# Gated attention: when the second half of a batch's softmax results is asked for

## The chip, the cores and the metric

One core of a Trainium2 chip. The metric is the time of one execution on the device in microseconds; lower is better. Five engines work side by side, each through its own instructions in order: PE (TensorE, matrix products), DVE (VectorE), ACT (ScalarE), POOL (GpSimd) and SP (SyncE), which computes nothing here and only issues transfers (DMAs). They wait for one another through semaphores.

## The reference

Two layers on 16 batches of 128 tokens with 512 features. The first is a decoder layer (self-attention, cross-attention, an MLP). The second, in whose part of the kernel the change lies, is a gated cross-attention:

```python
a = _layer_norm(audio_kv, ln_gamma, ln_beta)
Q = (hidden_states @ Wq.T) ...   # 16 heads of 32
K, V = (a @ Wk.T) ..., (a @ Wv.T) ...
scores = jnp.einsum('bhtd,bhsd->bhts', Q, K) * scale
scores = jnp.where(mask, scores, -inf)
attn = jax.nn.softmax(scores, axis=-1)
out = jnp.einsum('bhts,bhsd->bhtd', attn, V) @ Wo.T
return hidden_states + jnp.tanh(gate) * out
```

All of it is in float32.

## The kernel before, in words

The work goes in groups of four batches. Self-attention and cross-attention of all groups run first (one call of `attend`), then the MLP, then the gated attention of the four groups D0 to D3 (a second call of `attend`, with `ready=True`). The change is in `attend`; it acts in the second call only.

**Units and steps.** A batch has 16 heads and is cut into four *units* of four heads: unit `4b + j` is `j` of batch `b`, 64 units in the gated run. `attend` writes the instructions step by step, one unit a step, as a pipeline by hand. At step `k`:

- if `k` is a multiple of 4, PE computes the scores of a whole batch (`scores`, into four PSUM banks `sc`);
- DVE masks the scores into SBUF tiles `s` (`scale_unit`, tag `s`, seven buffers), one or two units a step, and finds each row's least value;
- ACT takes the exponentials of unit `k-1` (`exp_unit`), POOL divides unit `k-2` by its sums (`norm_unit`);
- DVE transposes unit `k-3` in squares of 32 and SP sends it to DRAM, 256 KB (`turn_unit`, tile `away_D<-s_D` in the trace);
- SP fetches a pair of units back in four pieces of 128 KB (`receive_pair`, tile `pT_D<-away_D`, tag `pT`, three buffers), which finishes the transposition: the squares land where they belong;
- PE mixes the values of a batch with its four units (`mix`, `av_D` in the trace), one of the two pairs being units `4b`, `4b+1`, the other `4b+2`, `4b+3`.

Each unit is thus sent at step `u + 3`. The dictionaries `mixed_at` and `received_at` say at which step a batch is mixed and a pair received. In the gated run a batch `b` is mixed at step `4b + 10`; its first pair is received at step `4b + 6` (the later unit of it was sent at `4b + 4`), and its second at `4b + 8` (later unit sent at `4b + 6`). The last batch (15) doesn't travel: its units are transposed by PE.

**Order inside a step.** What sets the order on SP is the order in which `step` calls things:

```python
if m == 0 and bt is not None:
    scores(bt)
for pair in pairs:
    receive_pair(*units[pair])
due()
...
for job in jobs:
    job()
...
    ahead.prepare(k % NS)
if 0 <= k - 3 < len(units) and not first_turned:
    (turn_unit if k - 3 < by_transfer(k) else turn_by_array)(*units[k - 3])
```

So a step's receive stands on SP ahead of that step's other transfers, and its send stands last. A receive waits until both sends of its pair have landed in DRAM. SP issues in order: whatever stands behind a waiting receive waits with it. The trace also shows that a DMA is issued only after the one eight places before it has landed (the back_x piece at 999.78 us is issued when the one of 995.10 has landed at 999.76, that of 1000.48 when that of 995.74 has).

**What else travels in the gated run.** While group `g` runs its attention, `jobs` projects Q, K and V of the next group on PE, and `prepare` (class `GatedAttention`) fetches the tokens of the group after that: `hidden_states` sends x turned (`turned_x`, steps 6, 8, 10, 12), and pieces of 256 KB come back at positions 1, 3 (`back_x`) and 7, 9 (`back_a`) of a group's 16 steps, two each time. ACT needs them at positions 5, 6 and 12 to 15. In the third group `deferred_start` fetches earlier groups' mixed results (`mixed`, positions 7, 9, 11, 13) and x (position 15); in the fourth the output is stored. `put_away` stores a mixed result (`kept_mT`), and each group loads a mask (`m`) before its first step.

Of the kernel before, what the change touches and what calls it, by code (L numbers as in the profile page):

```python
# [26 lines left out]
GB = 4  # L27
# [27 lines left out]
def decoder_then_gated_cross_attention(ctx: ExitStack, tc: tile.TileContext, a: dict, out: bass.AP):  # L55
# [24 lines left out]
    def afterwards(engine, do):  # L80
        late[engine].append(do)

    def due():

        left = [do for queue in (late["dve"], late["act"]) for do in queue]
        for queue in late.values():
            queue.clear()
        for do in left:
            do()
# [456 lines left out]
    def scores(bt):  # L546
        sec, t = bt.sec, slice(bt.b * S, (bt.b + 1) * S)
        for j in range(GB):
            bt.sc[j] = ps("sc", f"sc_{bt.name}_{j}")
        for c in range(KC):  # L550
            for j in range(GB):
                r = slice(j * HD, (j + 1) * HD)
                nc.tensor.matmul(
                    bt.sc[j][:, c * S : (c + 1) * S], sec.q[r, c, t], sec.k[r, c, t], start=True, stop=True
                )
# [4 lines left out]
    def by_head(t):  # L560
        return t.rearrange("p n c j -> p c n j")
# [30 lines left out]
    def norm_unit(bt, j):  # L592
        s, sm = bt.s[j], bt.sum.pop(j)
        nc.vector.reciprocal(sm, sm)
        scale = sm.unsqueeze(1).unsqueeze(3).to_broadcast([P, NQ, KC, Q])
        nc.gpsimd.tensor_tensor(s, s, scale, ALU.mult)
# [24 lines left out]
    def receive_pair(bt, j):  # L621

        pT = work.tile([P, NQ, 2, KC, Q], F32, tag="pT", name=f"pT_{bt.name}_{j}", bufs=3)
        for m in range(NQ):
            nc.sync.dma_start(
                out=pT[m * Q : (m + 1) * Q].rearrange("k n u c q -> k n (u c q)"),
                in_=bt.away[j // 2][m].rearrange("(n k) u x -> k n (u x)", k=Q),
            )
        for u in range(2):
            bt.pT[j - 1 + u] = pT[:, :, u]  # L630

    def mix(bt):
        sec, b = bt.sec, bt.b
        av = ps(mixed_in[0], f"av_{bt.name}")
        for c in range(KC):
            for j in range(GB):
                h = c * GB + j
                nc.tensor.matmul(
                    av[j * HD : (j + 1) * HD, c * S : (c + 1) * S], sec.v[:, b, h * HD : (h + 1) * HD],
                    bt.pT[j][:, :, c, :], start=True, stop=True,  # L640
                )
        at_end = work.tile([P, KC, S], F32, tag="s", name=f"mT_{bt.name}", bufs=7) if bt.by_array else None
        mT = bt.mT = sec.mixed_tile(b) if at_end is None else at_end

        def mixed_out():
            if sec.v_bias is None:
                nc.scalar.copy(mT, av.rearrange("p (c q) -> p c q", q=S))
            else:
                for c in range(KC):
                    nc.scalar.activation(  # L650
                        mT[:, c], av[:, c * S : (c + 1) * S], AF.Identity, bias=col(sec.v_bias[0], sec.v_bias[1] + c)
                    )

        return mixed_out

    def out_project_last(bt):

        for n in range(2):
            at_ = slice(n * HF, (n + 1) * HF)
            mm = ps("mm", f"mo_{bt.name}_{n}")  # L660
            for c in range(KC):
                nc.tensor.matmul(
                    mm[:, 0:HF], bt.mT[:, c, :], bt.sec.w_o[:, c, at_], start=(c == 0), stop=(c == KC - 1)
                )
            bt.sec.finish(mm[:, 0:HF], bt.b, at_)

    def out_project(bt):
        mm = ps(mixed_in[0], f"mo_{bt.name}")
        for c in range(KC):
            nc.tensor.matmul(mm, bt.mT[:, c, :], bt.sec.w_o[:, c, :], start=(c == 0), stop=(c == KC - 1))  # L670
        afterwards("dve", lambda: bt.sec.finish(mm, bt.b))
# [13 lines left out]
    def attend(sections, ready, others, after=None):  # L685

        if not ready:
            sections[0].start(sections[1])
        units, batches = [], []
        projected = deque()

        last = (len(sections) * GB - 1) * GB

        def by_transfer(n):

            return min(n, last) if ready else n  # L700

        mixed_at, received_at = {}, {}
        for b in range(len(sections) * GB):
            sooner = 2 if ready else min(2, max(0, b + 4 - len(sections) * GB))
            k, at = (b + 3) * GB - sooner, (b + 2) * GB - max(1, sooner)
            if ready and b * GB == last:
                k = last + 7
            else:
                for half in range(2):
                    received_at.setdefault(at + 2 * half, []).append(b * GB + 2 * half + 1)  # L710
            mixed_at[k] = b

        def step(k, bt=None, jobs=(), ahead=None):

            m = k % GB
            mixed_in[0] = "sc" if not ready and k > last + 2 else "mm"
            pairs, done = received_at.get(k, []), mixed_at.get(k)
            beside_scores = done is not None and m == 0
            if beside_scores:
                mixed_out = mix(batches[done])  # L720
# [5 lines that stand above are left out]
            if beside_scores:  # L726
                mixed_out()
                projected.append((k, batches[done]))
            for job in jobs:
                job()  # L730
            last_mix = ready and k == last + 7
            if last_mix:
                afterwards("act", mix(batches[-1]))
                projected.append((k, batches[-1]))
            if projected and k - projected[0][0] >= (1 if ready and bt is None else 2):
                before = projected.popleft()[1]
                if before.by_array:
                    out_project_last(before)
                elif before.sec.deferred:
                    afterwards("act", lambda: before.sec.put_away(before))  # L740
                else:
                    out_project(before)
            first_turned = ready and k == last + 6
            if first_turned:
                turn_by_array(*units[k - 3])
            if done is not None and not (beside_scores or last_mix):
                mixed_out = mix(batches[done])
                if ready:
                    afterwards("act", mixed_out)
                else:  # L750
                    mixed_out()
                projected.append((k, batches[done]))
            if ahead is not None:
# [3 lines that stand above are left out]
            def norm():  # L757
                if 0 <= k - 2 < len(units):
                    norm_unit(*units[k - 2])

            def exp():
                if 0 <= k - 1 < len(units):
                    least_unit(*units[k - 1])
                    exp_unit(*units[k - 1])


            for do in (exp, norm) if ready else (norm, exp):
                do()
            if bt is not None:
                for j in SCALED[m]:  # L770
                    scale_unit(bt, j)
                if bt.b < sec.by_head_from:
                    bt.sec.add_mask(by_head(bt.s[m]), bt.b)

        k = 0
        for i, sec in enumerate(sections):
            jobs = others() if i + 1 == len(sections) else sections[i + 1].jobs()
            ahead = sections[i + 2] if i + 2 < len(sections) else after if i + 2 == len(sections) else None
            for b in range(GB):
                bt = Batch(sec, b)  # L780
                batches.append(bt)
                for m in range(GB):
                    units.append((bt, m))
                    step(k, bt, jobs.get(k % NS, ()), ahead)
                    k += 1
        while projected or k < len(units) + 2 * GB:
            step(k, jobs=jobs.get(k - len(units) + NS, ()))
            k += 1
# [1038 lines left out]
```

## Time and profile before

| what | value |
|---|---|
| median of 3 runs | 1155.73 us (1155.29 to 1156.04) |
| the profiled execution | 1154.62 us |
| its span, first to last instruction | 1152.8 us |
| its granted TensorE clock | 0.997 |
| busy on PE, DVE, POOL, ACT | 98%, 64%, 60%, 53% of the span |
| queue 1 (all of SP's DMAs) | 258.38 MB, 78.8% of 16 engines' span |
| gated run, first scores to end of the span | 940.7 to 1152.8 us |

The profile is of one execution. Its busy shares say how long each engine worked; the lists of waits say what ended each engine's idle time; the timeline gives instructions in order with their start and length, runs of like ones merged ("x4"), and in brackets the idle time before and what ended it. A DMA's row on SP is the time its issue took; the transfer itself goes on, and the trace has the moment at which each landed.

Where a step of the gated run stands in time: the scores of batches 0 to 15 (steps 0, 4, 8 ...) start at 940.7, 952.4, 963.3, 976.5, 987.7, 1000.6, 1012.4, 1025.7, 1036.8, 1049.7, 1060.8, 1072.0, 1083.1, 1096.0, 1108.9 and 1120.0 us, so a step takes some 2.9 to 3.0 us.

### The profile page before, as it was taken

To read this page: it belongs to the slowest core of one execution; us is meant where nothing else is said; L and a number is where in the kernel's file an instruction comes from. 1 tells how busy PE (TensorE), PEld (TensorE's weight loads), DVE (VectorE), ACT (ScalarE), POOL (GpSimd) and SP (SyncE) were. 2 spreads that over 40 slices of the span, in tenths; PEclk is the share of its full clock that TensorE was granted. 3 is DMA by queue.
4 is the path that set the end of the run, shared out by engine and by line. 5 is a ranking of instruction groups with operands and counts; after the bars stand their busy time and mean duration, and the time that the engine had idled before them with its cause. 6 is when DMAs were issued, how large, how long until landed. Compare 5 with 4: busy or idle time off the path is not lost.

```text
span 1152.8 us, 22191 instructions
## 1 busy us (share of the span) xinstructions
PE 1129.9 (98%) x7246; PEld 873.1 (76%) x7246; DVE 743.4 (64%) x1919; ACT 611.1 (53%) x2142; POOL 694.6 (60%) x633
## 2 busy tenths in 40 slices
PE   9999999999999999999999999999999999999998
PEld 8877777666675757546788888888888877878875
DVE  6678978798787776987564634443342237767754
ACT  3567676767667666774231333233222337877663
POOL 6798888788868685773333414443342168545873
PEclk9999999999999999999999999999999999999999
DMA  6588889999888879999696696697447827888975
GB/s 222 159 211 233 217 221 224 256 240 260 210 225 217 233 217 250 289 285 294 226 258 234 183 283 191 201 274 261 155 154 228 261 59 201 236 253 230 267 220 175
DMA packets 325284, 259.81 MB, mean 225 GB/s; under 512 B 83560, under 2 KB 280624, under 8 KB 320304
## 3 DMA queue, kind: packets, MB, share of 16 engines
q1 hardware_dynamic: 325128, 258.38, 78.8%
q8 instruction: 58, 0.95, 0.4%
q14 instruction: 58, 0.48, 0.1%
q10 hardware_dynamic: 40, 0.01, 0.0%
HBM read 163.94 MB, written 94.37 MB: 224 GB/s over the span
## 4 chain that ended last, share of the span: by engine, by line
PE 71%; DMA 10%; POOL 6%; DVE 5%; ACT 3%; issue 3%; SPq 2%; POOLq 0%; DVEq 0%; ACTq 0%
PE h L51 17%; PE o L51 16%; PE mo_A L51 4%; PE mm_q_B L51 3%; PE mm_v_B L51 3%; PE mo_B L51 3%; PE mm_v_A L51 3%; PE mm_q_A L51 3%; PE mm_v_D L51 3%; PE mm_k_A L51 3%; PE mm_k_B L51 3%; PE mm_q_D L51 2%; DMA away_D<-s_D 2%; POOL x L51 2%; SPq L51 2%
## 5 line engine op out<-in xcount | busy, mean ns | idle before, releaser
L51 DVE TENSOR_TENSOR h<-h,h 128x512 f32<-128x512 f32 x80 | 54.9, 686 | 114.5 <-PE h L51 114.5
L51 ACT ACTIVATE h<-h 128x512 f32<-128x512 f32 x64 | 40.3, 630 | 161.5 <-DVE h L51 161.5
L51 ACT ACTIVATE s_A<-s_A,mn_A 128x128 f32<-128x128 f32 x256 | 99.4, 391 | 46.7 <-issue 24.1
L51 ACT ACTIVATE s_B<-s_B,mn_B 128x128 f32<-128x128 f32 x256 | 99.4, 392 | 31.1 <-issue 18.2
L51 POOL TENSOR_TENSOR s_D<-s_D,sum_D 128x512 f32<-128x512 f32 x64 | 66.5, 1040 | 57.7 <-DVE sum_D L51 52.2
L51 ACT ACTIVATE s_D<-s_D,mn_D 128x128 f32<-128x128 f32 x256 | 99.1, 392 | 0.4 <-issue 0.4
L51 POOL TENSOR_TENSOR s_B<-s_B,sum_B 128x512 f32<-128x512 f32 x64 | 67.1, 1048 | 52.2 <-DVE sum_B L51 38.1
L51 POOL TENSOR_TENSOR s_A<-s_A,sum_A 128x512 f32<-128x512 f32 x64 | 66.7, 1042 | 30.5 <-DVE sum_A L51 23.9
L51 POOL TENSOR_TENSOR s_A<-s_A,ma 128x512 f32<-128x512 f32 x64 | 81.9, 1280 | 5.1 <-DVE s_A L51 4.1
L51 POOL TENSOR_TENSOR s_B<-s_B,mask 128x512 f32<-128x512 f32 x60 | 76.6, 1277 | 2.2 <-DVE s_B L51 1.3
L51 POOL TENSOR_TENSOR rstd_aD<-rstd_aD,mhalf 128x1 f32<-128x1 f32 x12 | 6.6, 550 | 115.1 <-DVE rstd_aD L51 101.6
L51 POOL TENSOR_TENSOR sh<-h 128x512 f32<-128x512 f32 x32 | 40.6, 1270 | 50.6 <-ACT h L51 49.6
L51 PE MATMUL h<-sx,t 128*128 128x256 f32 x256 | 61.9, 386 | 2.0 <-ACT h L51 2.0
L51 PE MATMUL h<-T_C,w 128*128 128x256 f32 x256 | 61.1, 381 | 0.8 <-DVE h L51 0.8
L51 PE MATMUL h<-T_C,t 128*128 128x256 f32 x256 | 60.6, 379 | 1.0 <-DVE h L51 1.0
L51 PE MATMUL o<-w,h 128*128 128x256 f32 x256 | 60.9, 381 | 0.0
L51 PE MATMUL o<-t,h 128*128 128x256 f32 x256 | 60.5, 379 | 0.0
L51 PE MATMUL o<-t,sh 128*128 128x256 f32 x256 | 60.5, 379 | 0.0
L51 DVE CUSTOM_DVE_ANT_0 s_D<-sc_D,gmask 128x128 f32<-128x128 f32 x256 | 57.2, 283 | 2.1 <-DMA turned_x<-x_D 1.2
L51 PE MATMUL mo_B<-w_co,mT_B 128*128 128x512 f32 x128 | 57.6, 593 | 0.0
L51 PE MATMUL mo_A<-w_ao,mT_A 128*128 128x512 f32 x128 | 57.5, 592 | 0.0
L51 PE MATMUL mm_q_B<-T_B,w_cq 128*128 128x512 f32 x128 | 57.4, 596 | 0.0
(335 smaller groups left out, 3002.0 us busy)
## 6 DMA issues: line engine op xcount, KB each, us to landing
t<-kept SPq DMA_DIRECT2D x24, 1024.0 KB, 8.0
away_A<-s_A SPq DMA_DIRECT2D x64, 256.0 KB, 3.1
pT_A<-away_A SPq DMA_DIRECT2D x128, 128.0 KB, 3.5
away_B<-s_B SPq DMA_DIRECT2D x64, 256.0 KB, 4.5
pT_B<-away_B SPq DMA_DIRECT2D x128, 128.0 KB, 3.7
away_D<-s_D SPq DMA_DIRECT2D x60, 256.0 KB, 3.5
pT_D<-away_D SPq DMA_DIRECT2D x120, 128.0 KB, 2.7
w<-in_L_xattn_w_dram SPq DMA_DIRECT2D x24, 512.0 KB, 6.1
```

Of the source, the lines that this page charges most:

```text
L51: return lambda *args, **kw: self.tc.keep_in_program_order(call(*args, **kw))
```

## The change

One line in `attend`. In the gated run (`ready`), the second pair of a batch is received one step after the first instead of two: at step `4b + 7`, not `4b + 8`. That is seven units behind the scores of the batch and one step behind the send of the pair's later unit. The first pair, the mixing and everything else stay where they are; the first call of `attend` is unchanged.

```diff
             else:
                 for half in range(2):
-                    received_at.setdefault(at + 2 * half, []).append(b * GB + 2 * half + 1)
+                    received_at.setdefault(at + (1 if ready else 2) * half, []).append(b * GB + 2 * half + 1)
             mixed_at[k] = b
```

On SP the order between a batch's two receives changes from "first receive, send 4b+3, step 4b+7's transfers, send 4b+4, second receive, send 4b+5, send 4b+6" to "first receive, send 4b+3, second receive, step 4b+7's transfers, send 4b+4, send 4b+5, send 4b+6".

## The prediction

> **What bounds the kernel now.** I read the page's first part, then busy time by stage for the gated run (start 940.7 us, where the first of its scores run), then who waited for whom there on PE and on SP.
>
> ```profile
> PE 1129.9 (98%) x7246; PEld 873.1 (76%) x7246; DVE 743.4 (64%) x1919; ACT 611.1 (53%) x2142; POOL 694.6 (60%) x633
> ```
> ```profile
> 940.00:988.00 48.00, 46.27 (x373) 37.96 (x375) 33.97 (x172) 34.01 (x131) 39.61 (x34) 1.00 0.71 189
> 988.00:1037.00 49.00, 47.02 (x428) 38.69 (x425) 34.07 (x174) 37.12 (x153) 26.40 (x24) 1.00 0.92 249
> 1037.00:1083.00 46.00, 46.00 (x424) 38.26 (x423) 34.62 (x175) 33.67 (x148) 30.54 (x28) 1.00 0.88 244
> ```
> ```profile
> PE av_D L51 <- DMA pT_D<-away_D: 2.5, 4, 1.7
> PE tp_D L51 <- POOL s_D L51: 1.7, 1, 1.7
> ```
> ```profile
> SPq L51 <- DMA away_D<-s_D: 40.5, 28, 3.5
> SPq L51 <- DVE s_D L51: 31.0, 16, 9.8
> ```
>
> PE is the bound: in the gated run it idles about 6 us before its last matmul, and only 2.5 us of that is waiting for softmax results (av is the mix of batch b, at step 4b+10). The last two figures of a stage row are the share of the DMA engines and GB/s: 0.92 and 0.88 in the middle. The second bound is close behind: SP, which issues every DMA in order. Its receives waited 40.5 us, in 28 of 30 cases, for a send to land. It was on time (waiting for DVE to finish a unit) for 16 sends of 60.
>
> The four waits of PE, from its timeline, and SP's queue at the longest:
>
> ```profile
> 971.88 1.07 PE L51 MATMUL av_D<-pT_D,v_D__7856 128*32 128x128 f32 x28 [0.15 <-DMA pT_D<-away_D]
> 1009.49 1.07 PE L51 MATMUL av_D<-pT_D,v_D__7856 128*32 128x128 f32 x28 [0.26 <-DMA pT_D<-away_D]
> 1021.02 1.07 PE L51 MATMUL av_D<-pT_D,v_D 128*32 128x128 f32 x28 [1.72 <-DMA pT_D<-away_D]
> 1140.72 1.94 PE L51 MATMUL av_D<-pT_D,v_D 128*32 128x128 f32 x60 [0.33 <-DMA pT_D<-away_D]
> ```
> ```profile
> 1010.11 1.78 SPq L51 DMA_DIRECT2D pT_D<-away_D  x4
> 1011.99 0.38 SPq L51 DMA_DIRECT2D away_D<-s_D  x1
> 1012.41 1.01 SPq L51 DMA_DIRECT2D back_a<-turned_a  x2
> 1013.52 0.38 SPq L51 DMA_DIRECT2D away_D<-s_D  x1
> 1014.86 2.31 SPq L51 DMA_DIRECT2D pT_D<-away_D  x4
> 1017.28 0.38 SPq L51 DMA_DIRECT2D away_D<-s_D  x1
> ...
> 1021.54 1.73 SPq L51 DMA_DIRECT2D pT_D<-away_D  x4
> ```
> ```profile
> 1011.99 2.81 DMA away_D<-s_D
> ...
> 1016.74 4.04 DMA pT_D<-away_D
> 1021.02 1.07 PE av_D L51 x28
> ```
>
> Units are counted from 0; send n is that of unit n. The rows are batch 4: first receive, send 19, two pieces of the next group, send 20, second receive. The chain of waits (last fence) shows that send 19 landed at 1014.80 and that the second receive was issued at 1014.86, that is on landing. It could not have gone earlier.
>
> **The change, part by part.** No instruction is added, removed or resized on any engine. On SP alone, the four DMAs of each batch's second receive (15 times) move from the head of step 4b+8 to the head of step 4b+7: ahead of send 4b+4 and of whatever else step 4b+7 issues. That is two pieces of back_a or back_x in batches 0, 3 and 4; two of mixed or x in 8, 9 and 10; an output store in 13 and 14; the next mask in 2 and 6; nothing else in 1, 5, 7, 11 and 12. No other queue is passed.
>
> *What goes.* A second receive still waits for send 4b+3 to land, one step behind it now. Sends take 2.2/3.5/5.9 us to land (least, median, most, the tile view of s_D); a step is some 2.9 us. So it goes out hardly earlier; but its transfers overtake those it passed. In batch 4 these are three transfers of 256 KB, each seen to take about 0.7 us of a busy queue (landings 0.64 to 0.81 us apart where it was backed up): about 2 us sooner, which would end the 1.72 us wait. The 0.15 and 0.26 us would go likewise. The 0.33 us at the end would not: its receive (issued 1136.63) waited for send 59, landed 1136.58, and only a store was passed. The most that can be won is 2.1 us.
>
> *What comes.* Everything passed is now queued on SP behind the wait for a landing, plus the four issues (1.75 to 1.9 us). Before, that work filled the wait. Worked out on batch 0: send 3 went at 963.71 and landed at 966.36; two back_a pieces and send 4 (965.77) filled the gap; the receive went at 966.42, an x send at 968.29, send 5 at 968.83. After: the receive again at 966.42 to 968.24, then two pieces (1.1), send 4 at 969.4 (3.6 late), x send, send 5 at 970.3 (1.5 late). The DMA queue has nothing from 966.36 until the receive's first piece; send 5 lands about 974.8 instead of 973.04. The next receive waits for it: 1.8 late; sends 6 and 7 follow it; send 7's landing moves from 980.36 to 982.1, so batch 1's second receive lands at 986.3 instead of 984.50, where mix 1 started at 984.74. That is about 1.5 us on PE, which had none.
>
> Batch 4 the same way: receive at 1014.86, two pieces to 1017.8, send 20 some 4.3 late, send 21 about 1.1 late, the next receive at 1021.65 if the 2.4 us hold-up that the first back_a piece met (5.49 us to land) falls into the empty queue, at about 24.0 if not: 0.1 to 2.5 late. So a laden batch pushes SP back by 0.1 to 2.5 us; I take 1.5, near batch 0's 1.8. An unladen batch leaves the queue idle for about one transfer, 0.7 us.
>
> *The reserve.* From the landings of the second receives and the starts of the mixes, the margin was 0.2 us in batch 1, 1.3 in 2, none in 3 and 4 (they waited), 2.6 in 5, 1.8 to 2.7 in 6 and 7, 0.8, 1.4 and 1.5 in 8 to 10, 2.5 in 11, 3.2 or more in 12 and 13.
>
> *The sum.* Batches 0 to 3 push 1.8+0.7+1.5+1.8 = 5.8 us by mix 4; its own overtaking gives about 2 back, so some 3.8 us more waiting than before by then. Batch 4 pushes another 1.5: SP is 7.3 late at mix 5 against a margin of 2.6, so 4.7 in all; I take 4.5. Batches 5 to 7 recover. Batches 8 to 10 push 4.5, 11 another 0.7, against margins of 1.5 to 2.5: 3 us by mix 11. I add 1.5 for hold-ups that the reserve used to absorb, in the tail too. Together +9. The profiled execution took 1154.62 us (span 1152.8 and 1.8 around it), 1.1 below the median of 1155.73: 1163.6, so I say 1164. With 0.1 a laden batch nearly all fits the margins (within 2 us of before); with 2.5 the eight laden batches up to 10 push 1.0 more each, less some margin: +15.
>
> *A rule against the row.* The row: these sends, 256 KB, landed after 3.5 us in the median and 2.2 at least. The Trainium skill, DMA: Bandwidth & Descriptors, section "Anatomy of one DMA", has a fixed 2.0 us plus bytes over 436 GB/s (fitted on the GpSimd path): an estimate of 2.6 us. By it each wait would be 0.9 shorter, and a sum over these eight batches would lose some 7 of the 9 us. The same section calls the fixed part completion latency: a queue that is emptied before each receive pays it anew, which speaks against the change. The row is measured in this queue, so it decides.
>
> **The rivals.**
> - *SP becomes the bound in the laden stretches (forecast)*: +4 to +14 us. For it: late sends already (send 17 was turned at 1002.03 and issued at 1006.95). Against it: DVE's 31.0 us of SP waits show reserve in the last section. Chance 0.60.
> - *The late sends also block DVE (+14 to +22, 1172)*: a late send keeps its s buffer, one of seven, so the scaling seven units later waits on DVE, and scores, turns and sends with it. For it: DVE waited 1.2 us for an x send and 0.3 us for a send before such scalings (about 980 and 1005), and send 20 had 1.0 us to spare. Against it: margins of 2.5 us and more from batch 7 on. Eight batches at 1 us more: 1172. Chance 0.14.
> - *The passed work has time (not slower)*: send 4b+4 is first needed three steps later. It decides if the push of a laden batch stays under about 0.5 us, so that margins of 0.8 to 2.6 us take it: 1154 to 1157.5. For it: empty queues let transfers land in 2.2 us, and the hold-ups may fall into them. Chance 0.18, within 0.2% nearly all.
> - *All three avoidable waits go and nothing else comes*: 1155.73-2.1 = 1153.6, just within 0.2%; faster than that only if the 0.9 us PE waited for mn_D goes too. Chance 0.08, half of it faster.
>
> **How the numbers follow.** 0.2% (2.3 us) is about what a measurement of this kernel can tell from no change. Slower: 0.60+0.14+0.04 of the third = 0.78; within: 0.18; faster: 0.04. The range, 1154 to 1174, reaches from the third rival's low end to the second's price and leaves out 2 in 10 at most.
>
> **What the profile after would show.** Right: SP's wait for away_D over 50 us; each send 4b+4 two to eight us after its turn; PE waiting for pT_D about 10 us, at mixes 1, 3, 4 and 8 to 11; the gaps of the first mix gone. Wrong: PE's wait for pT_D below 3 us. If instead PE waits for mn_D before scores, and DVE for away_D, the second rival is at work. The stages before 940 us should not change.

## The result and the profile after

The changed kernel took 1167.72 us (median; 1166.72 to 1169.62 in 4 runs) beside 1155.88 us of the kernel before on the same chips: a ratio of 1.0111, 95% interval 1.0091 to 1.0132, slower by 11.8 us in the medians, 12.8 by the ratio. The profiled execution spans 1164.9 us where before's spanned 1152.8. PE's busy time is the same, its share one point lower:

```profile
PE 1130.7 (97%) x7246; PEld 872.2 (75%) x7246; DVE 743.1 (64%) x1919; ACT 611.8 (53%) x2142; POOL 695.3 (60%) x633
```

All of the loss is in the gated run: from its first scores to the end of the span it takes 225.0 us, 12.9 more than before's 212.1. Who waited there, on SP, PE, DVE and ACT (total us, times, longest):

```profile
SPq L51 <- DMA away_D<-s_D: 69.0, 33, 4.3
...
SPq L51 <- DVE s_D L51: 16.2, 6, 9.8
```
```profile
PE mm_k_D L51 <- ACT k_D L51: 5.3, 2, 4.6
PE sc_D L51 <- DVE mn_D L51: 2.0, 3, 0.9
PE mm_o_D L51 <- ACT mT_D L51: 1.8, 1, 1.8
PE av_D L51 <- DMA pT_D<-away_D: 1.4, 2, 0.8
PE tp_D L51 <- POOL s_D L51: 1.3, 1, 1.3
PE mm_v_D L51 <- DVE v_D L51: 1.2, 1, 1.2
PE mm_o_D L51 <- DVE x L51: 0.7, 1, 0.7
```
```profile
DVE s_D L51 <- DMA away_D<-s_D: 9.2, 6, 2.6
DVE x L51 <- DMA x<-kept_x: 6.4, 2, 4.9
```
```profile
ACT T_D L51 <- DMA back_x<-turned_x: 6.3, 1, 6.3
```

SP waits 69.0 us for sends to land (40.5 before) and waits for DVE, that is, is ahead of it, 6 times, not 16. (The counts are of single DMAs: two of before's 28 were not receives but transfers that waited for the DMA eight places before, so 26 belong to receives, not the 28 that the prediction read.) PE waits 13.9 us instead of 5.8, and hardly for pT_D: the 2.5 us of before became 1.4. It waits for ACT and for DVE, and these wait for transfers that SP issued late: DVE 9.2 us for sends that still hold an s buffer (0.3 before), ACT 6.3 us for a back_x piece (0.5 before, at the same place).

Against before's schedule (set equal at the first scores), the scores of batch 4 come 2.6 us late, of batch 6 9.5, of batch 13 11.0, of batch 15 12.6. The largest step, 7.0 us, lies between the scores of batches 5 and 6 (about 1002 to 1021 us), in which batch 4's results are received; it is called the block below. SP's timeline ahead of it, then the chain of work that leads to PE's longest wait, and that wait:

```profile
1000.91 1.73 SPq L51 DMA_DIRECT2D pT_D<-away_D  x4
1002.75 0.38 SPq L51 DMA_DIRECT2D away_D<-s_D  x1
1007.50 1.73 SPq L51 DMA_DIRECT2D pT_D<-away_D  x4
1009.28 0.90 SPq L51 DMA_DIRECT2D back_x<-turned_x  x2
1010.29 0.93 SPq L51 DMA_DIRECT2D away_D<-s_D  x2
```
```profile
1002.75 4.70 DMA away_D<-s_D
...
1009.75 4.29 DMA back_x<-turned_x
...
1015.17 1.63 ACT s_D L51 x8
1016.80 0.48 ACT k_D L51
...
1017.42 3.75 PE mm_k_D L51 x8
```
```profile
1017.42 3.75 PE L51 MATMUL mm_k_D<-T_a,gsums 128*128 128x256 f32 x8 [4.62 <-ACT k_D L51]
```

Send 15 goes at 1002.75. Batch 3's second receive stands behind it now, and SP does nothing for 4.4 us until it has landed. Two back_x pieces, sends 16 and 17 follow at 1009.28 to 1011.2; send 16 had been turned at 1001.42. ACT, in order, stands before the back_x piece from 1007.8 to 1014.1, its exponentials and the copy of k_D behind it; PE wants the bank that this copy frees and idles 4.62 us. Then PE's clock is halved; busy time by stretch (the figure ahead of the last two is the granted clock):

```profile
1016.00:1018.00 2.00, 0.58 (x2) 0.52 (x3) 1.16 (x10) 2.00 (x8) 0.91 (x1) 0.50 0.80 239
1018.00:1022.00 4.00, 4.00 (x24) 2.90 (x26) 2.00 (x4) 3.13 (x13) 1.17 (x2) 0.50 0.55 150
```

The halved stretch lasts 6.83 us (1015.4 to 1022.2); eight matmuls took 3.75 us, not 1.99. Had PE worked all through it, that would be 3.4 us of work lost; PE was idle until 1017.4, so some 2.4 us are. Waits (+8.1) and clock (+2.4) make 10.5 of the 12.9; the rest was not followed.

### The profile page after: what moved, and what is told of

The parts are those of the page before. It is cut to its first block, busy times and chain, and to the rows that moved or that the text cites. A ratio compares the mean times of both kernels' runs of the same rounds, so it can differ in the third digit from the quotient of the medians.

```text
span 1164.9 us, 22210 instructions
## 1 busy us (share of the span) xinstructions
PE 1130.7 (97%) x7246; PEld 872.2 (75%) x7246; DVE 743.1 (64%) x1919; ACT 611.8 (53%) x2142; POOL 695.3 (60%) x633
```

## The experiments

Each edit is against the kernel after, in the line of the diff or near it; times stand beside the kernel before on the same chip, and a loss in us is worked out from the ratio (on about 1156 us). Two theories stood first: A and B both made the block the heart of the loss, the rival C a general lateness that shows where it happens to.

**Only batch 3 moved.**
```diff
-received_at.setdefault(at + (1 if ready else 2) * half, [])...
+received_at.setdefault(at + (1 if ready and b == 3 else 2) * half, [])...
```


> Only batch 3's second receive moves to step 4b+7; the other 14 stay at 4b+8. In the changed kernel ACT waited 6.3 us for the back_x pieces that this receive passes, and PE idled 4.6 us behind it at half clock afterwards. Theory A (the wait is made by lateness that SP gathers over batches 0 to 3, and the passed pieces only hand it to ACT): SP is on its old schedule here, send 15 lands near 1005 as before, the pieces go out about 1007 and land about 1010.3 where ACT wanted them at 1009.7: 0 to +2 us, about 1157. Theory B (the passed pieces alone are the cause): the whole block at 1011 to 1022 returns, +6 to +9 us, about 1163.

1160.29 us beside 1156.19, ratio 1.0046 (1.0028 to 1.0064): about 5 us, between A and B. In its profile ACT waits 3.4 us for back_x, PE 2.83 us behind it, and the clock is halved for 3.41 us:

```profile
ACT T_D L51 <- DMA back_x<-turned_x: 3.4, 1, 3.4
```

The passed pieces hurt even with SP on its old schedule up to there, so the block is real. By the time between the scores of batches 5 and 6 it is 3.3 us in this profile, less than half of the changed kernel's 7.0; the profiled execution was the fastest of six, 1157.25 us. The expectation under A reckoned from a wrong moment. ACT needs all of back_x at position 5, and before the change it already stood waiting for the last piece there:

```profile
1006.60 1.15 ACT L51 ACTIVATE T_D<-back_x 128x512 f32<-128x512 f32 x2 [0.55 <-DMA back_x<-turned_x]
```

So ACT wanted the pieces by 1006.6 at the latest, not at 1009.7 as the expectation had it, and a landing at 1010.3 is some 3.7 us late, about what ACT waits here.

**All but batch 3 moved.**
```diff
+received_at.setdefault(at + (1 if ready and b != 3 else 2) * half, [])...
```


> The change in every batch but 3, whose second receive stays at step 4b+8, behind the back_x pieces. Theory A: SP is still 2 to 4 us late by batch 3, but ACT gets its pieces before the late receive, so the 4.6 us idle of PE and the halved clock go, and some waiting for pT_D comes at mixes 3 and 4 in their place: +4 to +7 us, about 1161. Theory B: only what lies outside the block is left, +3 to +5 us, about 1160. Rival C (every late send costs DVE and PE about the same in each batch, the block is no more than where it shows): nearly nothing is won, +10 to +12 us.

1166.10 us, ratio 1.0101 (1.0079 to 1.0124): 11.7 of the 12.8 us stay, and the difference is within the noise. The 4.6 us wait for k_D is gone (0.7 us is left, as before the change), and others have its place:

```profile
PE av_D L51 <- DMA pT_D<-away_D: 6.4, 5, 1.7
PE sc_D L51 <- DVE mn_D L51: 2.4, 3, 1.1
```

A and B, which made the block the heart of the loss, fall; C's range holds the result. The block takes up lateness that costs about the same elsewhere when it cannot come out there.

**Pieces asked for earlier.**
```diff
-            if p in (1, 3, 7, 9):
+            third = 2 if g == 3 else 3
+            if p in (1, third, 7, 9):
                 for m in range(2):
-                    self.part(m + 2 * (p in (3, 9)))
+                    self.part(m + 2 * (p in (third, 9)))
```


> The changed kernel, with the second two back_x pieces of group 3 asked for one step earlier (position 2 of 16 instead of 3), so that batch 3's receive no longer passes them; they stand ahead of send 15 instead. All 15 receives stay at 4b+7. Theories A and B: ACT's wait of 6.3 us for back_x goes, PE's 4.6 us behind it too, and the halved clock: about +5 us left of the 12, 1160 to 1162. Rival C: 1166 to 1168, since SP has the same work in a slightly other order.

1170.89 us, ratio 1.0139 (1.0116 to 1.0162), if anything worse than the change itself. ACT no longer waits for back_x, but send 15 now follows two more pieces, and PE waits 3.4 us for pT_D at mix 3, with 6.83 us at half clock behind it. A and B fall again; C comes nearest, but the time lies above its range too, and where the excess comes from was not followed.

**The step's other transfers first.**
```diff
-            for pair in pairs:
-                receive_pair(*units[pair])
+            behind = ready and m == GB - 1
+            if not behind:
+                for pair in pairs:
+                    receive_pair(*units[pair])
             due()
...
                 ahead.prepare(k % NS)
+            if behind:
+                for pair in pairs:
+                    receive_pair(*units[pair])
```


> All second receives stand in step 4b+7, but behind the other transfers of that step and ahead of send 4b+4 alone. So the pieces of back_a, back_x, mixed and x fill SP's wait for the landing again; only send 4b+4 is late. Theory A: an unladen batch's push (0.7 us) is left in every batch, less than the margins of the second receives: +0 to +4 us, about 1158. Rival C, in the form that the late sends hold the s buffers and so DVE: send 4b+4 is as late as in the changed kernel, +8 to +12 us.

1160.74 us, ratio 1.0047 (1.0028 to 1.0067): 5.4 of the 12.8 us are left, between the two expectations. More than half of the loss goes when the pieces, masks and stores are no longer passed; what is left comes with sends 4b+4 alone. C in its DVE form is not borne out here: DVE waits 8.1 us for sends, nearly the 9.2 of the changed kernel, but PE's wait for DVE's mn_D is the 0.9 us of before, and PE waits for pT_D instead, 5.2 us at seven mixes.

Theory D came out of these: what costs is SP standing before a landing with nothing left to issue, 15 times, each time about a send's whole landing.

**First receive later, second as before the change.**
```diff
+received_at.setdefault(at + (1 + half if ready else 2 * half), [])...
```


> The second receive back at step 4b+8 as before the change; instead the first receive moves one step later, from 4b+6 to 4b+7. Both its sends have landed by then, so it waits for nothing, and its four issues (1.8 us) and send 4b+4 fill the time in which send 4b+3 lands, for which the second receive waits. Theory D (what costs is SP standing empty-handed in front of a landing, so that sends and pieces behind it run late): SP's wait for sends falls from 40.5 to under 20 us, the 2.5 us that PE waited for pT_D shrink to under 1, nothing else on PE changes: 0.1 to 0.2% faster than before, about 1154.5. Rival E (each receive has a margin of its own, and the first pair's was needed): PE waits more for pT_D, 0 to +4 us.

1156.83 us beside 1155.22, ratio 1.0017 (1.0004 to 1.0029). Slightly slower, where theory D expected slightly faster. SP's wait fell much further than expected, yet the time did not:

```profile
SPq L51 <- DVE s_D L51: 59.2, 32, 9.8
SPq L51 <- DMA away_D<-s_D: 4.9, 9, 1.7
```
```profile
PE av_D L51 <- DMA pT_D<-away_D: 3.4, 2, 2.7
```

At mix 0 PE waits 2.7 us: batch 0's second receive now has the first one and two back_a pieces ahead of it, and its margin was none. E was right at this one place, and SP's wait is not the only thing that counts.

**Both receives at step 4b+7.**
```diff
+received_at.setdefault(at + (1 if ready else 2 * half), [])...
```


> The second receive at step 4b+7 as in the changed kernel, and the first receive at the same step, just ahead of it. The second receive passes just what it passes in the change, but the first one's 1.8 us of issues now fill most of its wait, and sends 4b+3 go out without a receive ahead of them. Theory D: SP's wait for sends is 20 to 35 us, below the 40.5 of before, and the time is that of before within 3 us (1154 to 1159). Rival F (what costs is that the pieces and send 4b+4 stand behind the second receive, whatever SP does meanwhile): they are as late as in the change or later, +8 to +14 us.

1156.01 us, ratio 1.0002 (0.9987 to 1.0017): no loss, with every second receive where the change put it. This decides against F, which expected +8 to +14 us. D's time holds; its figure for SP's wait, 20 to 35 us, was too high. SP's timeline around batch 0, and its waits:

```profile
963.19 0.36 SPq L51 DMA_DIRECT2D away_D<-s_D  x1
963.65 3.87 SPq L51 DMA_DIRECT2D pT_D<-away_D  x8
967.62 0.85 SPq L51 DMA_DIRECT2D back_a<-turned_a  x2
968.57 0.38 SPq L51 DMA_DIRECT2D away_D<-s_D  x1
```
```profile
SPq L51 <- DMA away_D<-s_D: 8.7, 10, 1.9
```

Here send 4 goes at 968.57, in the changed kernel at 968.55: in batch 0 it is about as late after its turn, 3.3 us (3.6 there). In batch 1 send 8 is again 3.3 us late, where the changed kernel has 5.2. Send 4b+7 goes 0.1 us after its turn in nearly all batches, since no receive stands before it, and nothing adds up. Two things changed together here: SP's wait is filled with issues, and each send 4b+3 goes ahead of the first receive. No run separates them. What is left in PE's waits is 1.6 us for DVE before the scores of batch 3 and 2.3 us for ACT behind back_x; none is for pT_D.

**Only batch 4 moved.**
```diff
+received_at.setdefault(at + (1 if ready and b == 4 else 2) * half, [])...
```


> Only batch 4's second receive moves to step 4b+7. It was issued on the landing of send 19 before and would be still, but ahead of two back_a pieces and send 20, so it should land about 2 us sooner and end the one long wait of PE for pT_D (1.72 us) if nothing is gathered behind it. By the prediction's account of one batch: 1 to 1.7 us faster than before, 0.1%. By a general account in which any moved receive costs about a fifteenth of the loss: +0.8 us.

1154.25 us beside 1155.22, ratio 0.9994 (0.9981 to 1.0007): not to be told from before, and neither account is excluded. In the profile the 1.72 us wait of mix 4 is gone, and mix 5 waits 1.3 us, which had waited for nothing: what was won is given back one batch later.

**The five batches that pass send 4b+4 alone.**
```diff
+received_at.setdefault(at + (1 if ready and b in (1, 5, 7, 11, 12) else 2) * half, [])...
```


> The change only in batches 1, 5, 7, 11 and 12, whose step 4b+7 issues nothing but send 4b+4. By the prediction's terms each pushes SP by 0.7 us against margins of 0.2 us (batch 1) and 2.5 us or more (the others): 0 to +2 us. If every moved receive costs alike, a third of the loss: +4 us.

1156.19 us, ratio 1.0008 (0.9989 to 1.0027), in the range of the first account; a third of the whole loss (+0.37%) is excluded. A third of what others_first lost (1.8 us, +0.16%), where too only sends 4b+4 are passed, is not. So the run shows that these five cost less than their share of the whole, and not whether that is because they pass little or because unmoved receives stand between most of them. Batch 3 alone, a single moved receive, cost 5 us.

**First receive later, except in batch 0.**
```diff
+received_at.setdefault(at + (1 + half if ready and b else 2 * half), [])...
```


> As first_later (first receive at step 4b+7, second at 4b+8), but batch 0 keeps its order of before (4b+6 and 4b+8). In first_later PE waited for pT_D twice: 2.7 us at mix 0, whose second receive had the first one and two back_a pieces ahead of it, and 0.75 us at mix 4. With batch 0 as before, 0.15 and about 0.8 us should be left of the 2.5 us of before: 1 to 1.5 us faster than before, 0.1%, about 1154. Rival: margins further on shrink as PE runs ahead of SP again, and 1 to 2 us of waiting come back at mixes 3 and 4: no difference.

1153.96 us beside 1156.42, ratio 0.9983 (0.9967 to 1.0000): in the profile the wait at mix 0 is gone, 1.1 us are left at mix 4. As expected, but at the edge of what can be told.

**Both at 4b+7, except batch 0 and batch 3's second.**
```diff
+received_at.setdefault(at + (1 + half * (b == 3) if ready and b else 2 * half), [])...
```


> Both receives of a batch at step 4b+7 as in both_at_seven, but batch 0 as before (4b+6, 4b+8) and batch 3's second receive at 4b+8, behind the back_x pieces for which ACT waited 2.9 us in both_at_seven. There PE waited 1.6 us for DVE before the scores of batch 3 (send 4 late, batch 0's) and 2.3 us for ACT behind back_x, and not at all for pT_D. If those two are the whole of its loss: no wait of PE for pT_D and 1.6 to 2.4 us faster than before, 0.15 to 0.2%, about 1153.5. Rival: late sends 4b+4 of batches 1, 2 and 4 hold s buffers, DVE waits for them, and the time is that of before.

1152.19 us beside 1156.42, ratio 0.9966 (0.9951 to 0.9981): faster than both kernels. All that PE still waits for in the gated run:

```profile
PE tp_D L51 <- POOL s_D L51: 1.8, 1, 1.8
PE sc_D L51 <- DVE mn_D L51: 0.9, 1, 0.9
PE mm_k_D L51 <- ACT k_D L51: 0.7, 1, 0.7
```

No mix waits for pT_D any more, at the end neither. The profiled gated run is 3.3 us shorter than before's, 2.5 of them the waits for pT_D.

## Why the prediction was right, and where it was not

- **The bound (SP close behind PE, bound after the change): right.** SP's wait for sends was to pass 50 us and is 69.0; sends 4b+4 were to leave two to eight us after their turn and left 3.6 to 8.9 after it. both_at_seven shows that the new place alone does not cost anything: the second receives pass the same transfers there, SP waits 8.7 us for sends, and there is no loss.
- **"It goes out hardly earlier": right.** Batch 0's second receive went at 965.76, 0.66 us before its time of before; the whole gated run started 0.78 us earlier.
- **The working on batch 0: right up to the mix.** Send 4 was to be 3.6 late and left 3.58 after its turn; send 5, 1.5 late, was 1.5 late. The next receive was 2.4 late, not 1.8. But mix 1 did not wait 1.5 us: PE had first waited 0.9 us for DVE before the scores of batch 3, which moved the mix too.
- **"PE waiting for pT_D about 10 us, at mixes 1, 3, 4 and 8 to 11": wrong.** It was 1.4 us, at mix 3 and in the tail, and the prediction itself had named a wait below 3 us as the sign of being wrong. The step that failed is the reserve: I measured what SP's lateness costs by one customer, the mix, and priced the passed pieces only as SP's time. ACT needs all of back_x at position 5 and had no reserve there (it waited 0.55 us for it before the change); DVE needs the s buffers back. They are in-order engines with PE's next operand behind, and they held PE up first: 5.3 us for ACT's k_D, 3.2 for DVE's mn_D and v_D. The mixes, delayed with them, then had time. In all_but_batch3, pieces_early and others_first, where ACT is mostly spared, the waits for pT_D do come (6.4, 5.2 and 5.2 us). So the total came near by another road than the one forecast, and that is in part luck.
- **The waits of the first mixes: half right.** The 0.15 us is gone as forecast, batch 0's transfers landing 1.0 us sooner (measured from the first scores, as below), and the last wait stayed (0.33, now 0.59). The 1.72 us of mix 4 is gone for another reason: its transfers land 5.7 us later than before, and the mix comes later still. The 0.26 us of mix 3, which was to go, became 0.78.
- **The sum: +9, measured +11.8.** An unladen push of 0.7 us, held by the margins, seems too small for the row of 15: others_first, which leaves only sends 4b+4 to pass, still lost 5.4 us (+0 to +4 was expected of it), and SP's wait for sends is 59.6 us there, 1.3 a batch more than before. The halved clock (some 2.4 us) was not in the sum at all.
- **The second rival (late sends block DVE): partly at work.** DVE waited 9.2 us for sends, 3.2 us of PE's waits are for DVE's mn_D and v_D (0.9 before). A kernel with more s buffers was not tried, so how much of the loss goes by this way is not shown.
- **The price of the Trainium skill** (DMA: Bandwidth & Descriptors, "Anatomy of one DMA", by whose figures the prediction estimates 2.6 us a landing, and most of the loss would vanish) differs from the trace: send 15 took 4.7 us, batch 0's send 3 took 2.8, and the loss is there.

Left open: how the 12.9 us divide between ACT's and DVE's way. Blocking one moves the lateness to another, so the parts do not add up.

## What to carry to other kernels

A wait on the queue that issues all transfers is paid by everything behind it, so count what the queue has to issue while it waits, and put a transfer that is already free to go into that time: here the same early receive cost 12 us alone and nothing that could be measured once the first receive stood just ahead of it, with the sends in front of both. When a queue runs late, look for the customer with the least margin on every engine, not only for the one whose transfer was moved. A saved wait counts only if the next batch does not give it back.

## What the runs showed of the hardware

Gaps of some two to five us in PE's work were followed by half its clock, but not all of them. In others_first a gap of 1.93 us was followed by 3.41 us at half clock (granted clock by stretch):

```profile
1020.00:1022.60 2.60, 0.67 (x13) 0.37 (x16) 2.04 (x11) 1.02 (x6) 1.93 (x3) 1.00 1.04 269
1022.60:1026.00 3.40, 3.40 (x33) 2.66 (x26) 2.21 (x11) 0.59 (x1) 2.28 (x3) 0.51 1.05 275
```

In only_batch3 it was 2.83 us, with 3.41 at half clock; in the changed kernel 4.62, with 6.83. Gaps of 1.72 (before), 2.32 (both_at_seven) and 2.66 us (first_later) brought none. So a gap of about 2 us costs either itself or up to 1.7 us more (half of 3.41), and the halved stretches seen here behind such gaps last 3.41 us or twice that. What decides whether a gap of 2 to 3 us halves the clock stays open: its length alone does not.
